# Involution: neighbourhoods laid out by the host and loaded raw, group norm applied behind the product

## The chip, the cores and the metric

The kernel runs on one core of a Trainium2 chip. The metric is the time on the device of one execution, in microseconds (us). The engines named below are PE (TensorE, matrix products), DVE (VectorE), ACT (ScalarE), POOL (GpSimd) and SP (SyncE, which here only issues DMAs). All data are 32-bit floats.

## The reference

Two layers on x of 8 images, 256 channels and 56 x 56 pixels. The first is an involution behind a group norm; the second is a block of two 3 x 3 convolutions with ternary weights and batch norms. The change lies in the first:

```python
ker = einsum('bchw,oc->bohw', gn(x), w_reduce) + b_reduce      # 256 -> 64
ker = einsum('bchw,oc->bohw', ker, w_span) + b_span            # 64 -> 16 * 49
xp = pad(gn(x), 3)
patches = stack([xp[:, :, i:i+H, j:j+W] for i in range(7) for j in range(7)])
x = x + (ker.reshape(B, 16, 1, 49, H, W)
         * patches.reshape(B, 16, 16, 49, H, W)).sum(axis=3)   # 16 groups of 16 channels
x = x + block(gn(x))                                           # the convolutions
```

Here `gn(v) = (v - m) / sqrt(s + 1e-5)`, with mean m and variance s of each image and each group of 8 channels. Every pixel has its own 7 x 7 kernel for each of 16 groups.

## The kernel before

The first stage works through 32 quarters (`quarters`, L984): an image b and 64 of its channels, c. The 128 partitions of a quarter are these 64 channels of the upper and of the lower half of the image, in the tile `xs[b, c]`. A quarter has ten rows of tiles (`ty`), each row seven tiles (`TX`) of 3 x 8 pixels (`PY`, `PX`) in both halves. A tile with its border is 9 x 14 = 126 pixels (`NQ`).

The product is done on PE with the pixels of the neighbourhood as the rows that are summed over. `q` is a tile of 126 neighbourhood pixels by 7 tiles by 128 channels. `a` (two buffers) holds for the same 126 pixels the kernels of each of the 24 output pixels, zero where the pixel lies outside its 7 x 7. `apply_row` (L861) makes one row with 28 products of `q` and `a`, and `pick_out` (L881) takes the channels of the right group out of its result (ACT L887, DVE L888, where `half_sb` is 1 or 0) and adds it to `xs` (POOL L891).

`generate` (L821) fills `a` for the next quarter, in 14 units: PE multiplies shifted windows of `wl` with `kr`, the reduced input (L842); `UNITS` says how many of a unit's positions ACT moves out of PSUM with the bias (L846), and DVE moves the rest (L851). `reduce` (L700) computes `kr` for the next image.

`q` needs the normalised pixels on partitions, while `xs` has the channels there. It comes in two ways. For four of the seven tiles (`NK`), `prep` (L755) writes the normalised input with its border to `xn` (POOL, `spread`, L734), transposes it on PE (L777), copies it to `stg` (ACT L780) and stores it in DRAM in `xtd` (SP L768); `load_q` (L797) loads 126 pixels by 512 values from there (SP L802). For the other three (`NX`), `surround` (L738) writes the bordered input to `xe` (POOL), with three rows of the other half from the host in `xa` (SP L743), and `transpose_q` (L805) transposes on PE (L809) and copies to `q` (ACT L812). The border must be zero after the norm; `xn`, `xe` and the ends of `xtd` are zeroed once.

The order on each engine is that of the text: `pin` (L924) ties every instruction to the one before it on its engine. In a row SP issues, in turn: stores of a finished quarter (`store_x1`, L903) or loads of the next image (L605), the stores that wait in `tasks`, then after `apply_row` the `load_q` that takes the buffer which this row frees (four buffers, `NQB`), and later the pieces of the convolutions' weights, which are quantised beside this stage (L294 loads, L323 stores to `wqd`). SP can't pass a DMA whose wait is not over.

After this stage come both convolutions (`conv_phase`, L355, with the products at L521) and an elementwise last stage (L1112).

## Time and profile before

| | |
|---|---|
| time before, median of 3 runs | 2253.05 us (2248.57 to 2256.51) |
| the profiled execution's own span | 2247.9 us |
| PE busy over the span | 1849.4 us (82%) |
| DVE busy | 1757.2 us (78%) |
| ACT busy | 1252.6 us (56%) |
| POOL busy | 580.1 us (26%) |
| moved by DMA | 411.28 MB |

The profile comes from one execution. A group of instructions is a line of the code with its engine, operation and tiles; beside it stand the number of instructions, the busy time, the mean time of one in ns, and the idle time of the engine just before them with what ended it. Busy times overlap between engines, so they don't add up to the span. In the waits, "SPq L802 <- PE pa L875" is time in which the DMA queue of SP stood at the DMA of L802 until an instruction of L875 on PE was done: total, times, longest. In a table of stretches each engine has its busy time and number of instructions in that stretch; then come the granted clock of PE (1.00 is full), the mean busy share of the 16 DMA engines, and GB/s.

### The profile page before, as it was taken

How to read it: one execution, taken by the hardware profiler on the slowest of the kernel's cores; microseconds unless marked ns; L12 is line 12 of the kernel's file. 1: busy time of each engine (PE TensorE's matmuls, PEld its weight loads, DVE VectorE, ACT ScalarE, POOL GpSimd, SP SyncE). 2: the span in 40 equal slices, each digit the busy share in tenths (PEclk: the TensorE clock that was granted, in tenths of full speed). 3: DMA queues.
4: the chain of work that ended last, by engine and by line, in shares of the span. 5: the costliest groups of instructions: out<-in, count | busy, mean ns of one | idle time of the engine just before them, and what ended most of it. 6: DMA issues, size and time to landing. Idle time of an engine off the chain costs nothing. (4 is left out here: it accounts for less than half of the span.)

```text
span 2247.9 us, 73156 instructions
## 1 busy us (share of the span) xinstructions
PE 1849.4 (82%) x31088; PEld 1701.1 (76%) x31088; DVE 1757.2 (78%) x3246; ACT 1252.6 (56%) x2417; POOL 580.1 (26%) x1320
## 2 busy tenths in 40 slices
PE   5989898898989889889889999999899999980000
PEld 4777777777877777778789999999899999980000
DVE  6767867678686776856589999998999999985444
ACT  3545555454554545556546766665576666663434
POOL 3536455464554645546400000000000000000000
PEclk9999999999999999999989999999899999995555
DMA  6647658475475755755453333334333333369999
GB/s 201 191 109 212 183 135 223 112 220 175 143 218 132 209 155 162 211 131 164 145 189 123 144 138 121 117 117 169 149 117 117 117 117 117 117 247 409 430 429 400
DMA packets 187588, 411.28 MB, mean 183 GB/s; under 512 B 77311, under 2 KB 93565, under 8 KB 179837
## 3 DMA queue, kind: packets, MB, share of 16 engines
q1 hardware_dynamic: 181664, 376.57, 51.3%
q10 hardware_dynamic: 5596, 30.03, 3.2%
q8 instruction: 245, 4.01, 0.8%
q14 instruction: 83, 0.67, 0.1%
HBM read 264.05 MB, written 142.48 MB: 181 GB/s over the span
## 5 line engine op out<-in xcount | busy, mean ns | idle before, releaser
L521 PE MATMUL c<-pl,wq 128*128 128x392 f32 x4608 | 858.1, 349 | 17.8 <-ACT pl L391 17.8
L521 PEld LDWEIGHTS c<-pl,wq 128*128 128x128 f32 x4608 | 856.1, 190 | 19.6 <-ACT pl L391 18.3
L851 DVE TENSOR_TENSOR a<-pg,bt 126x756 f32<-126x756 f32 (+3 forms) x640 | 392.2, 655 | 158.8 <-ACT a L846 122.4
L842 PE MATMUL pg<-kr,wl 64*126 64x140 f32 (+1 forms) x6144 | 447.6, 288 | 24.5 <-DVE a L851 14.2
L842 PEld LDWEIGHTS pg<-kr,wl 64*126 64x126 f32 x6144 | 385.2, 190 | 75.7 <-issue 42.8
L875 PE MATMUL pa<-a,q 126*32 126x48 f32 x17920 | 271.9, 207 | 61.9 <-issue 38.2
L875 PEld LDWEIGHTS pa<-a,q 126*32 126x32 f32 x17920 | 221.6, 111 | 115.2 <-issue 52.7
L846 ACT ACTIVATE a<-pg,bt 126x126 f32<-126x126 f32 x768 | 243.8, 476 | 98.4 <-PE pg L842 98.2
L891 POOL TENSOR_TENSOR x<-x,inv 128x168 f32<-128x168 f32 x320 | 165.8, 519 | 444.3 <-DVE inv L888 402.2
L391 ACT CAST pl<-r 128x812 fp32r<-128x812 f32 x192 | 162.5, 867 | 144.2 <-DVE r L386 125.9
L812 ACT COPY q<-ptq 126x384 f32<-126x384 f32 x320 | 138.3, 482 | 161.5 <-issue 91.7
L888 DVE SCALAR_TENSOR_TENSOR inv<-pa,half_sb,inv 128x168 f32<-128x168 f32 x320 | 116.6, 365 | 134.9 <-ACT inv L887 116.4
L371 POOL MEMSET xp<- 128x116 f32 x32 | 6.2, 195 | 828.0 <-DVE a L386 828.0
L392 DVE TENSOR_TENSOR pl<-r,pl 128x812 fp32r<-128x812 f32 x192 | 187.1, 1001 | 29.3 <-ACT pl L391 28.1
L734 POOL TENSOR_SCALAR xn<-x,gn 128x224 f32<-128x224 f32 (+2 forms) x384 | 175.5, 478 | 113.5 <-PE pt L777 62.2
L456 ACT ACTIVATE dummy<-y,nc 128x1568 f32<-128x1568 f32 (+1 forms) x128 | 200.1, 1563 | 4.8 <-DVE y L541 3.5
L734 POOL TENSOR_SCALAR xe<-x,gn 128x168 f32<-128x168 f32 (+2 forms) x384 | 161.5, 440 | 0.0
L780 ACT COPY stg<-pt 98x512 f32<-98x512 f32 x128 | 75.1, 587 | 131.5 <-issue 94.0
L150 DVE BATCH_NORM_STATS2 st<-x 128x6 f32<-128x392 f32 x256 | 138.3, 556 | 12.9 <-DMA x<-in_x 11.3
L809 PE MATMUL ptq<-ident_sb,xe 128*126 128x128 f32 x960 | 143.2, 284 | 6.0 <-DVE var_a L170 5.0
L887 ACT ACTIVATE inv<-pa,half_sb 128x168 f32<-128x168 f32 x320 | 128.5, 402 | 27.7 <-PE pa L875 24.9
L1071 ACT ACTIVATE xp<-raw,gn 128x392 f32<-128x392 f32 (+1 forms) x124 | 82.6, 721 | 62.6 <-DVE a L386 59.0
(153 smaller groups left out, 1896.6 us busy)
## 6 DMA issues: line engine op xcount, KB each, us to landing
q<-xtd SPq DMA_DIRECT2D x320, 252.0 KB
raw<-x1d SPq DMA_DIRECT2D x32, 812.0 KB
raw<-y1d SPq DMA_DIRECT2D x32, 812.0 KB
x<-in_x SPq DMA_DIRECT2D x64, 392.0 KB
xtd<-stg SPq DMA_DIRECT2D x128, 196.0 KB
x1d<-x SPq DMA_DIRECT2D x64, 392.0 KB
y1d<-y SPq DMA_DIRECT2D x30, 784.0 KB
y2d<-y SPq DMA_DIRECT2D x30, 784.0 KB
```

The costliest lines, as they stand in the source:

```text
L150: nc.vector.bn_stats(st[:, j, :], xt[:, j * NC:(j + 1) * NC])
L391: nc.scalar.copy(hi, r)
L392: nc.vector.tensor_tensor(lo, r, hi.bitcast(F32), ALU.subtract)
L456: nc.scalar.activation(dst, v, f, bias=shift[:, to:to + 1], accum_out=stats[:, to, j, n:n + 1])
L521: nc.tensor.matmul(ps[:, to, :NM], wq[k][:, t, dx, to * P:(to + 1) * P], part[:, t, :, dx:dx + W], start=(c == 0), stop=(c == last))
L734: nc.gpsimd.tensor_scalar(dst[:, i - d - k0:f - d - k0, :, x0:x0 + n], v[:, i:f, :, j0:j0 + n], scale, bias, ALU.mult, ALU.add)
L809: nc.tensor.transpose(pt[:NQ, k * P:(k + 1) * P], xe[c % 2][:, k, PY * ty:PY * ty + QY].rearrange("p r x -> p (r x)"), ident_sb)
L842: nc.tensor.matmul(dst, wl[rows, c, gp, o:o + NQ], kr[py][rows, px, :], start=True, stop=True)
L846: nc.scalar.activation(whole[:, g0 + i, p0 + j], ps[:NQ, i, j * nt:(j + 1) * nt], AF.Identity, bias=bt[:, c, g0 + i, p0 + j:p0 + j + 1])
L851: nc.vector.tensor_tensor(dst[:, g0:g0 + 2, p0:p0 + nv].rearrange("q g p t -> q g t p"), ps[:NQ, :, t0 * nv:t1 * nv].rearrange("q i (t p) ...
L875: nc.tensor.matmul(ps[o:o + 32, k * 2 * n:(k + 1) * 2 * n], q[:NQ, k, o:o + 32], av[:, t + k, g * 2 * n:(g + 1) * 2 * n], start=True, stop ...
L891: nc.gpsimd.tensor_tensor(xv, xv, iv.rearrange("p t (y x) -> p y t x", x=PX), ALU.add)
```

## The change

The host now lays out the neighbourhoods themselves: `x_nb` holds, for each quarter, raw input with a zero border, by column and row of the neighbourhood and then seven tiles by 128 channels. `load_q` loads all seven tiles of a row in one DMA (3584 B for each of 126 pixels). `prep`, `spread`, the old `surround`, `transpose_q`, `xtd`, `xn`, `xe` and `xa` are gone. The pixels of a neighbourhood are now counted by column first.

As `q` is raw, the norm is put behind the product. The scale is a factor in `pick_out` (`scale2` in place of `half_sb`). The mean gives a term for each pixel: minus mean times scale, times the sum of the pixel's 49 weights. `constant` makes it once for each quarter, as the first two steps of `generate`: the weights summed over 49 (`wsx`, and `bsum` for the bias; summed once at the start from `w_all` and `b_all`) times `kr` on PE, scale and shift on ACT, and an add to `xs` on POOL. A border pixel must then hold the channel's group mean: `params` makes a tile `rim` of means, and `load_rim` copies it with DMAs from SBUF to the border of each `q` after its load. There are two for the left and right columns of every row, and one more for each image row that lies outside, at `ty` = 0, 8 and 9. The new `surround` issues them when more than two loads (`PLEAD`) are without their border. `NQB` is 5 instead of 4, `ps_p` has three buffers instead of two, with `ps_one` in the buffers of `pa`, and in `UNITS` ACT takes ten positions of 24 instead of six.

```diff
@@ -40,27 +40,22 @@
 NE = 2 * TX
 QY, QX = PY + K - 1, PX + K - 1
 NQ = QY * QX
-LEAD = (PY - 1) * QX + PX - 1
+LEAD = (PX - 1) * QY + PY - 1
 WL = LEAD + NQ
-NK = 4
-NX = TX - NK
 HQ = TY * PY + K - 1
-RP = NK * P
-SR = HH // 4
-NSP = SR * QX
-UNITS = ((0, 3, 0), (3, 3, 0), (6, 2, 0), (8, 4, 2), (12, 4, 1), (16, 4, 2), (20, 4, 1))
+UNITS = ((0, 3, 0), (3, 3, 0), (6, 2, 0), (8, 4, 3), (12, 4, 2), (16, 4, 3), (20, 4, 2))
 NU = GP * len(UNITS)
 A_COLS = (NT * NP + NE * PX) * GQ
-PER_ROW = (2, 1, 2, 1, 2, 1, 2, 1, 2, 0)
-NQB = 4
-QLEAD = 2
+PER_ROW = (2, 2, 2, 1, 2, 2, 1, 2, 2, 0)
+NQB = 5
+PLEAD = 2
 NCB = 4
...
@@ -576,14 +571,14 @@
     with ExitStack() as ph1:
-        ps_p = ph1.enter_context(tc.tile_pool(name="ps_p", bufs=2, space=PSUM))
+        ps_p = ph1.enter_context(tc.tile_pool(name="ps_p", bufs=3, space=PSUM))
         ps_a = ph1.enter_context(tc.tile_pool(name="ps_a", bufs=2, space=PSUM))
...
         def ps_one(name):
-            return ps_a.tile([P, 512], F32, tag="pt", name=name)
+            return ps_a.tile([P, 512], F32, tag="pa", name=name)
...
@@ -618,17 +613,23 @@
             dst = small.tile([P, NCQ, 2], F32, tag="gn1", name=f"gn1_{b}")
-            yield from group_norm_params(mvs.pop(b), dst, ps_one, f"a{b}")
+            means = []
+            yield from group_norm_params(mvs.pop(b), dst, ps_one, f"a{b}", means)
...
-            edge = small.tile([P, 2, NCQ], F32, tag="gn1e", name=f"gn1e_{b}")
+            scale2 = small.tile([P, NCQ, 2], F32, tag="gn1s", name=f"gn1s_{b}")
             for j in range(2):
-                nc.vector.tensor_scalar(edge[:, j], dst[:, :, 1], side_sb[:, j:j + 1], None, ALU.mult)
-            prm[b], prm_edge[b] = dst, edge
+                nc.vector.tensor_scalar(scale2[:, :, j], dst[:, :, 0], half_sb[:, j:j + 1], None,
+                                        ALU.mult)
+            shift = small.tile([P, NCQ], F32, tag="gn1b", name=f"gn1b_{b}")
+            nc.vector.tensor_tensor(shift, dst[:, :, 1], bsum, ALU.mult)
+            dg = work.tile([P, NCQ, P], F32, tag="dg", bufs=1, name=f"dg_{b}")
+            for c in range(NCQ):
+                nc.gpsimd.tensor_scalar(dg[:, c], ident_sb, means[0][:, c, 0:1], None, ALU.mult)
             yield
             yield
             ps = ps_one(f"br_{b}")
@@ -638,6 +639,12 @@
                                      start=(c == 0), stop=(c == NCQ - 1))
             yield
             nc.vector.tensor_tensor(brn, br, ps[:, :1], ALU.add)
+            ps = ps_one(f"rim_{b}")
+            nc.tensor.matmul(ps[:NQ, :NCQ * P], ones[:, :NQ], dg.rearrange("p c f -> p (c f)"),
+                             start=True, stop=True)
+            rim = small.tile([P, NCQ, P], F32, tag="rim", name=f"rim_{b}")
+            nc.scalar.copy(rim[:NQ].rearrange("p c f -> p (c f)"), ps[:NQ, :NCQ * P])
+            prm[b] = dst, scale2, shift, rim
         def gn2_params(b0, b1):
...
@@ -666,7 +673,8 @@
-        xn = fixed([P, NK, SR, QX], "xn")
+        wsum, wsx = fixed([P, G], "wsum"), fixed([P, NCQ, CH], "wsx")
+        bsum, ones = fixed([P, NCQ], "bsum"), fixed([P, P], "ones")
@@ -677,19 +685,7 @@
-        side_sb = fixed([P, 2], "side_sb", side)
-        nc.gpsimd.memset(xn, 0.0)
-        xe = [fixed([P, NX, HQ, QX], f"xe{i}") for i in range(2)]
-        for v in xe:
-            nc.gpsimd.memset(v, 0.0)
-        zero = xn.rearrange("p k r x -> p (k r x)")
-        for d in (d for ds in xt_d for d in ds):
-            for r0, n in ((0, PAD), (PAD + HH, HQ - PAD - HH)):
-                e = n * QX * RP // P
-                nc.sync.dma_start(
-                    bass.AP(d[:].tensor, d[:].offset + r0 * QX * RP, [[e, P], [1, e]]), zero[:, :e])
+        nc.gpsimd.memset(ones, 1.0)
         nf = CT * 9 * C
...
-        def spread(dst, src, k0, nk, scale, bias):
...
-        def surround(b, c):
-            dst, p = xe[c % 2], prm[b]
-            around = work.tile([P, 2, PAD * W], F32, tag="xa", bufs=1, name=f"xa_{b}_{c}")
...
-        def prep(b):
...
-                for s in range(HH // SR):
-                    spread(xn, xs[b, c][:, s * SR * W:(s + 1) * SR * W], 0, NK,
-                           prm[b][:, c, 0:1], prm[b][:, c, 1:2])
-                    yield
-                    pt = ps_one(f"pt_{b}_{c}_{s}")
-                    for k in range(NK):
-                        nc.tensor.transpose(pt[:NSP, k * P:(k + 1) * P],
-                                            xn[:, k].rearrange("p r x -> p (r x)"), ident_sb)
-                    stg = work.tile([P, NK, P], F32, tag="stg", name=f"stg_{b}_{c}_{s}")
-                    nc.scalar.copy(stg[:NSP].rearrange("p k c -> p (k c)"), pt[:NSP, :RP])
-                    tasks.append(lambda stg=stg, s=s, store=store: store(stg[:NSP], PAD + s * SR))
...
         def load_q(b, c, ty):
             q = qpool.tile([P, TX, P], F32, tag="q", name=f"q_{b}_{c}_{ty}")
-            d = xt_d[b % 2][c][:]
-            src = bass.AP(d.tensor, d.offset + PY * ty * QX * RP, [[RP, NQ], [1, RP]])
-            nc.sync.dma_start(q[:NQ, :NK].rearrange("p k c -> p (k c)"), src)
+            nc.sync.dma_start(q[:NQ].rearrange("p k c -> p (k c)"),
+                              x_nb[b, c, :, PY * ty:PY * ty + QY, :])
             return q
-        def transpose_q(b, c, ty):
-            pt = ps_one(f"ptq_{b}_{c}_{ty}")
-            for k in range(NX):
-                nc.tensor.transpose(
-                    pt[:NQ, k * P:(k + 1) * P],
-                    xe[c % 2][:, k, PY * ty:PY * ty + QY].rearrange("p r x -> p (r x)"), ident_sb)
-            nc.scalar.copy(loads[b, c, ty][:NQ, NK:].rearrange("p k c -> p (k c)"),
-                           pt[:NQ, :NX * P])
+        def load_rim(b, c, ty):
+            q, rim = loads[b, c, ty], prm[b][3][:, c]
+            e = PAD * QY
+            for k, r0 in ((0, 0), (TX - 1, NQ - e)):
+                nc.sync.dma_start(q[r0:r0 + e, k], rim[r0:r0 + e])
+            for h in range(2):
+                for r in range(QY):
+                    y = h * HH + PY * ty + r - PAD
+                    if 0 <= y < H or r >= K - 1 + min(PY, HH - PY * ty):
+                        continue
+                    cols = slice(h * CH, (h + 1) * CH)
+                    nc.sync.dma_start(q[r:NQ:QY, :, cols],
+                                      rim[:QX, cols].unsqueeze(1).to_broadcast([QX, TX, CH]))
...
                     a[:NQ, n:].rearrange("q (t f) -> q t f", t=NE))
+        def constant(b, c):
+            n = (TY - 1) * TX
+            add = work.tile([P, NHW], F32, tag="add", bufs=1, name=f"add_{b}_{c}")
+            rows_of = [v[:, :(TY - 1) * PY * W].rearrange("p (t y w) -> p y t w", y=PY, w=W)
+                       for v in (add, xs[b, c])]
+            last = [v[:, (TY - 1) * PY * W:] for v in (add, xs[b, c])]
+            scale, bias = prm[b][0][:, c, 1:2], prm[b][2][:, c:c + 1]
+            for i0 in (0, 2):
+                ps = ps_tile(f"ks_{b}_{c}_{i0}")
+                for i in range(2):
+                    py = (i0 + i) % PY
+                    k0, m = (0, n) if i0 + i < PY else (NT, TX)
+                    rows = slice(i * CR, (i + 1) * CR)
+                    for h in range(2):
+                        nc.tensor.matmul(ps[h * CH:(h + 1) * CH, i, :PX * m], wsx[rows, c, :],
+                                         kr[py][rows, :, k0 + h * m:k0 + (h + 1) * m],
+                                         start=True, stop=True)
+                for i in range(2):
+                    py = i0 + i
+                    m = n if py < PY else TX
+                    src = ps[:, i, :PX * m]
+                    if py < PY:
+                        dst = rows_of[0][:, py].rearrange("p t (k x) -> p t k x", x=PX)
+                        src = src.rearrange("p (x t k) -> p t k x", x=PX, k=TX)
+                    else:
+                        dst = last[0].rearrange("p (k x) -> p k x", x=PX)
+                        src = src.rearrange("p (x k) -> p k x", x=PX)
+                    nc.scalar.activation(dst, src, AF.Identity, bias=bias, scale=scale)
+                for i in range(2):
+                    py = i0 + i
+                    v, x_ = (r[:, py] for r in rows_of[:2]) if py < PY else last
+                    nc.gpsimd.tensor_tensor(x_, x_, v, ALU.add)
+                yield
         def generate(b, c, a):
+            yield from constant(b, c)
             whole, rest = (v.rearrange("q t (g p) -> q g p t", g=GQ) for v in views(a))
             for u in range(NU):
                 gp, (p0, n, na) = u // len(UNITS), UNITS[u % len(UNITS)]
...
@@ -884,20 +850,26 @@
                          [:, :, h] for h in range(2))
             inv = work.tile([P, TX, NP], F32, tag="inv", bufs=3, name=f"inv_{b}_{c}_{ty}")
             iv = inv[:, :, :n]
-            nc.scalar.activation(iv, even, AF.Copy, scale=half_sb[:, 0:1])
-            nc.vector.scalar_tensor_tensor(iv, odd, half_sb[:, 1:2], iv, ALU.mult, ALU.add)
+            scale = prm[b][1][:, c]
+            nc.scalar.activation(iv, even, AF.Copy, scale=scale[:, 0:1])
+            nc.vector.scalar_tensor_tensor(iv, odd, scale[:, 1:2], iv, ALU.mult, ALU.add)
             y, m = ty * PY, n // PX
             xv = xs[b, c][:, y * W:(y + m) * W].rearrange("p (y t x) -> p y t x", t=TX, x=PX)
             nc.gpsimd.tensor_tensor(
                 xv, xv, iv.rearrange("p t (y x) -> p y t x", x=PX), ALU.add)
         queue = [(b, c, ty) for b in range(B) for c in range(NCQ) for ty in range(TY)]
-        loads = {}
+        loads, bare = {}, []
         def prefetch():
             if queue:
                 k = queue.pop(0)
                 loads[k] = load_q(*k)
+                bare.append(k)
+        def surround(keep=PLEAD):
+            while len(bare) > keep or bare and not queue:
+                load_rim(*bare.pop(0))
...
+        held = []
         qpool = ph1.enter_context(tc.tile_pool(name="qpool", bufs=NQB))
         pieces = ph1.enter_context(tc.tile_pool(name="pieces", bufs=1))
+        for _ in range(2):
+            held.append(qpool.tile([P, TX, P], F32, tag="q", name=f"sums{len(held)}"))
+        wv, bv = (t_.rearrange("p k c -> p (k c)")[:, :n_ * KK]
+                  for t_, n_ in zip(held, (G, NCQ)))
+        nc.sync.dma_start(wv, w_all)
+        nc.sync.dma_start(bv, b_all)
+        for dst, v in ((wsum, wv), (bsum, bv)):
+            nc.vector.tensor_reduce(dst, v.rearrange("p (g k) -> p g k", k=KK), AX.X, ALU.add)
+        nc.vector.tensor_copy(wsx.rearrange("p c (g i) -> p (c g) i", g=GQ),
+                              wsum.unsqueeze(2).to_broadcast([P, G, CH // GQ]))
         pin(start=True)
         for _ in params(0):
             pass
-        strips, around = prep(0), surround(0, 0)
...
         for py in range(PY):
-            next(strips)
-            transfer(len(tasks))
             reduce(0, py)
             for _ in range(2):
                 next(found)
+        for _ in range(NQB):
+            prefetch()
+        surround(0)
         for u, _ in enumerate(generate(0, 0, a_next)):
-            if u < 4 or u % 3 == 0 and u < 12:
-                next(strips)
-                transfer(len(tasks))
-            elif u < 9:
-                next(around)
             next(found, None)
             pin()
-            if u == 5:
-                for _ in range(NQB):
-                    prefetch()
-        for _ in around:
-            pass
         for _ in found:
             pass
...
@@ -1012,20 +982,12 @@
...
-                transfer(2)
                 row = apply_row(b, c, a, ty)
+                surround()
                 prefetch()
                 if r == PARAMS_AT:
                     norm = params(b + 1) if more else gn2_params(0, b)
-                if more and r == STRIPS_AT:
-                    strips = prep(b + 1)
-                if ty % 2:
-                    next(strips, None)
-                if ty % 2 == 0:
-                    for k in rows[m * TY + ty + QLEAD:m * TY + ty + QLEAD + 2]:
-                        transpose_q(*k)
                 next(norm, None)
                 if ty == 1 and last is not None:
...
@@ -1145,30 +1104,38 @@
                                     .reshape(B, NCQ, P, -1))
     xh = np.asarray(x)
-    around = np.zeros((B, C, 2, 2, PAD, W), np.float32)
-    around[:, :, 0, 1], around[:, :, 1, 0] = xh[:, :, HH:HH + PAD], xh[:, :, HH - PAD:HH]
+    xp = np.zeros((B, C, HQ + HH, TX * PX + K - 1), np.float32)
+    xp[:, :, PAD:PAD + H, PAD:PAD + W] = xh
+    s = xp.strides
+    near = np.lib.stride_tricks.as_strided(
+        xp, (B, NCQ, QX, HQ, TX, 2, CH),
+        (s[0], CH * s[1], s[3], s[2], PX * s[3], HH * s[2], s[1]))
...
-        "x_around": by_quarter(around),
+        "x_nb": np.ascontiguousarray(near).reshape(B, NCQ, QX, HQ, TX * P),
```

## The prediction

> **What bounds the kernel now.** I read the page first, then the busy time by stretches, the groups of instructions, and last the waits of the DMA queue (SP). The page's chain of waits has L521 of the convolutions and the DMAs of the last stage on it; the change touches neither. What changes is the involution stage, from the first L875 matmul at 61.5 us to the last at 1131.8: 32 quarters of ten rows, 1070.3 / 32 = 33.45 us a quarter.
>
> ```profile
> core 0: us, PE busy (x) PEld busy (x) DVE busy (x) ACT busy (x) POOL busy (x), PEclk, DMA share, GB/s
> 61.50:1131.80 1070.30, 955.65 (x26128) 816.04 (x26126) 768.73 (x2039) 572.40 (x1565) 550.91 (x1235) 0.98 0.61 171
> ```
>
> Per quarter, each divided by 32: PE 29.9, DVE 24.0, ACT 17.9, POOL 17.2 us. PE is busy 89% of the stage and is the bound; the DMA engines are 61% busy. The groups that the change touches:
>
> ```profile
> L842 PE MATMUL pg<-kr,wl 64*126 64x140 f32 (+1 forms) x6144 | 447.6, 288 | 24.5 <-DVE a L851 14.2
> L846 ACT ACTIVATE a<-pg,bt 126x126 f32<-126x126 f32 x768 | 243.8, 476 | 98.4 <-PE pg L842 98.2
> L891 POOL TENSOR_TENSOR x<-x,inv 128x168 f32<-128x168 f32 x320 | 165.8, 519 | 444.3 <-DVE inv L888 402.2
> L812 ACT COPY q<-ptq 126x384 f32<-126x384 f32 x320 | 138.3, 482 | 161.5 <-issue 91.7
> L780 ACT COPY stg<-pt 98x512 f32<-98x512 f32 x128 | 75.1, 587 | 131.5 <-issue 94.0
> L809 PE MATMUL ptq<-ident_sb,xe 128*126 128x128 f32 x960 | 143.2, 284 | 6.0 <-DVE var_a L170 5.0
> ...
> L777 PE MATMUL pt<-ident_sb,xn 128*98 128x128 f32 x480 | 77.3, 284 | 0.0
> ```
>
> (The last line is from the groups of PE in that stretch.) The reader is to see that transposes cost PE 143.2 + 77.3 us, and ACT copies 213 us behind them. SP issues every DMA of this stage in order, and its own waits are these:
>
> ```profile
> SPq L802 <- PE pa L875: 413.4, 185, 8.2
> SPq L294 <- DMA wqd<-piece_w: 103.9, 50, 4.5
> SPq L768 <- ACT inv L887: 50.0, 64, 1.2
> SPq L802 <- PE ptq L809: 23.3, 37, 1.9
> ```
>
> SP is early: at L802 it waits for PE to give a q buffer back, 413.4 + 23.3 us here and 21.3 more in two smaller rows (PE pg 15.6, PE pt 5.7), 458 in all, or 14.3 us a quarter. That is SP's reserve. A DMA costs SP:
>
> ```profile
> L802 SPq DMA_DIRECT2D q<-xtd x320: 307/323/2186, 49.0 to 1127.5; - x160
> ...
> L768 SPq DMA_DIRECT2D xtd<-stg x192: 307/521/2118, 34.3 to 1072.0; - x192
> ...
> L743 SPq DMA_DIRECT2D xa<-in_x_around x32: 356/368/1706, 48.5 to 1084.9; - x32
> ```
>
> (min/median/max ns.) What the DMA engines give, in three short stretches (columns as in the first fence): x loads of 3136 B rows; q loads alone, 2048 B rows; the start of a wqd store of 192 B pieces.
>
> ```profile
> 4.00:5.00 1.00, 0.00 (x0) 0.00 (x0) 0.21 (x1) 0.00 (x0) 0.00 (x0) 1.00 1.08 387
> 394.00:394.40 0.40, 0.40 (x53) 0.40 (x47) 0.40 (x3) 0.40 (x2) 0.00 (x0) 1.00 0.82 312
> 398.00:398.40 0.40, 0.40 (x9) 0.40 (x10) 0.40 (x2) 0.40 (x2) 0.00 (x0) 1.00 0.63 61
> ```
>
> And how long after the issue data can be used: wf is issued in two halves, and DVE gets the first at 29.35. The stretches of 1 us from 25 on moved 157, 369, 396 and 433 GB/s, so a half's 1.18 MB were there near 28.6, and about 0.75 us went on completion.
>
> ```profile
> 24.01 0.93 SPq L698 DMA_DIRECT2D wf<-in_w  x2
> ...
> 29.35 0.95 DVE L223 TENSOR_REDUCE cols<-wf 128x1 f32<-128x768 f32 x1 [3.93 <-DMA wf<-in_w]
> ```
>
> [...] The wf loads agree in kind (0.75 us after the last byte, and a q load issued at 408.58 moves its first bytes in the stretch 409.2 to 409.6, 0.6 to 1.0 us later).
>
> **The change, part by part,** per quarter, against the profiled run's 33.45 us.
>
> PE, removed: 30 ptq transposes at 143.2 / 960 = 0.149 us (4.5 us) and 16 pt at 77.3 / 480 = 0.161 (2.6), in all 7.1. Added: the term `constant`, six matmuls of 504 columns and two of 56, f32, 64 rows deep. L842 takes 447.6 / 6144 x 2 = 0.146 us for 140 columns (two instructions each, two row halves side by side), so 504 columns take 0.53 and the sum is 3.3 us; if four run side by side (row halves and column halves), half of it. I take 2.5, range 1.6 to 3.3. PE goes from 29.9 to 25.3.
>
> DVE: ACT takes ten of 24 positions instead of six. The 756-element form has a mean of 958 ns and the 504 form 679, 1.06 to 1.1 ns an element; four 756 pieces become 504 and four 504 become 252, so 8 x 0.27 = 2.2 us less. ACT: 16 more evacuations at 243.8 / 768 = 0.32 (5.1) and three activations of 504 elements near 0.7 (kr at L716 is 738 ns for 560) plus one small, 2.4; less 213.4 / 32 = 6.7 of copies. Together +0.8, 18.7. POOL loses 30 L734 operations (960 / 32) near 0.42 and gets three adds of 504 elements near 1.2 and a small one, about -8.6. None of the three becomes the bound, and all of them lie beside PE.
>
> So the engines alone would allow 25.3 / 0.89 = 28.4, or 25.3 plus today's 3.55 of PE idle time = 28.9. I take 28.9: 4.55 less. The third pair of PSUM banks helps PE by at most the 36 us in which L842, L875 and L711 wait for DVE a.
>
> SP, removed: six xtd stores at 0.52 to 0.7 (the tail up to 2.1 lifts the mean), their 1.8 us of waits on ACT (50.0 and 6.3, over 32), one xa at 0.37: 5.3 to 6.5, I take 5.9. Added: 20 rims of 27 partitions near 0.33 (6.6) and eight row rims of 14x7 pieces near 0.52 as xtd's edge stores (4.2): 10.8. And a wait that is not there today: at ty = 8, 9 and 0 the row rims overlap the two side rims, so L742 waits until both have landed; so 3 times a quarter SP stands still. Queued behind it are the next q load, x loads, x1d stores and piece fetches. Not seen in the trace, so from both sides: [...] 0.8 + 0.2 + 0.75 = 1.8 us (first byte, transfer, completion); with a q load and another transfer still ahead, 3.5. The q load is issued right before, so I take 2.6: 7.8. Net 10.8 + 7.8 - 5.9 = 12.7 more. SP's work without its reserve is 33.45 - 14.3 = 19.15 today and then 31.85 us a quarter, more than the 28.9 of PE. So where PE's stall goes, SP is late next.
>
> DMA engines: a q load grows from 252 to 441 KB[...]. x loads give 387 / 16 / 1.0 = 24.2 GB/s an engine[...]. Per row also x 0.21, x1d 0.25 (319 GB/s in the stretch 410.4 to 410.8), wqd 0.3, pieces 0.1. [...] I keep 31.85.
>
> Start: the 16 zero fills (11.18 us of SP) and the strips go, the loads of five rows and w_all come; the opening waits for the statistics and `kr` in both. I take 3 us less (0 to 8). Convolutions and last stage: nothing.
>
> Sum: 32 x 1.6 = 51, and 3: 2247.9 - 54 = 2194. The median of the runs, 2253.05, stands 5.15 above the profiled span: 2199.
>
> **The rivals.** (A) as above, 2199; its own range is 2140 to 2240 (a wait of 2.0 to 3.0). (B) SP hides it all: each wait is 1.6 or less, or the lead of two rows (5.8 us) absorbs the late rows; PE decides: 32 x 4.55 + 3 = 149, 2104. For it: SP waits 43% of the time today. Against: 28 DMAs more. (C) No change to be told from noise, a wait near 3.1. (D) Slower: the wait for side rims is 3.5, since the q load of 441 KB and often an x1d or wqd transfer lie ahead[...]. At 3.1 SP's reserve is used up; at 3.5 the quarter takes 33.45 - 14.3 + 10.8 + 10.5 - 5.9 = 34.55, 32 x 1.1 - 3 = +32, 2285. For it: [...] SP's issues already reach 2.1 us[...]; also PE's clock was 0.50 in the stretch 406.0 to 407.6 of today's trace, so gaps could cost twice. That the change doesn't do what it says is out: neither L777 nor L809 is left in its order of instructions.
>
> **Numbers.** Chances: A 0.40, B 0.17, C 0.06, D 0.37. The range of 2095 to 2300 takes in B and most of D; about 0.2 lies outside. A alone: 2140 to 2240. A difference under 0.3% (7 us) can't be told from none. Faster 0.57, same 0.06, slower 0.37.
>
> **What would show it.** Right: no L809/L777; PE busy falls by about 4.6 us a quarter; SP's wait for PE falls from 14.3 us a quarter to near nothing, with waits of L742 for DMA q of 2 to 3 us, 96 times; PE waits for DMA q at rows 8, 9 and 0. B: SP still waits for PE several us a quarter. D: a DMA share over 0.8 and PE idle over 8 us a quarter. Wrong altogether: if PE waits for ACT a or DVE a, or if the convolutions' time differs.

## The result, and the profile after

| | before | after |
|---|---|---|
| time, median of 4 runs each, taken together | 2250.81 us (2243.54 to 2256.51) | 2739.47 us (2736.0 to 2742.39) |
| ratio after to before | | 1.2173 (95% interval 1.2129 to 1.2217) |
| span of the profiled execution | 2247.9 us | 2734.2 us |
| involution stage, first to last product (L875, now L841) | 61.5 to 1131.8 us | 66.8 to 1620.6 us |
| one quarter (stage / 32) | 33.45 us | 48.56 us |

The kernel became 22% slower, and the forecast was 2199 us, 2.3% faster. "Side rims" are the two transfers a row that fill the left and right columns of the border; "row rims" are the eight a quarter that fill the lines outside the image, at `ty` = 8, 9 and 0. Of the 486 us that the span grew, 483.5 lie in the involution stage (1553.8 instead of 1070.3 us), so everything below is told per quarter. First the stretch of that stage in the kernel after (columns as in the prediction's first fence: length, busy time of each engine, granted clock of PE, DMA share, GB/s):

```profile
66.80:1620.60 1553.80, 973.54 (x25203) 796.41 (x25202) 741.24 (x2051) 583.36 (x1759) 306.25 (x473) 0.79 0.54 146
```

No engine is full: PE is busy 63% of the stage, DVE 48%, the DMA engines 54%. The clock fell from 0.98 to 0.79. So the stage waits for something that is not compute. The groups of instructions say for what (busy us, mean ns; then idle time ahead of the group and what ended it):

```profile
L841 PE MATMUL pa<-a,q 126*32 126x48 f32 x17920 | 329.1, 228 | 540.3 <-DMA q<-rim 479.6
...
L808 PE MATMUL pg<-kr,wl 64*126 64x140 f32 (+1 forms) x6144 | 489.6, 312 | 17.3 <-DVE a L817 10.5
...
L812 ACT ACTIVATE a<-pg,bt 126x126 f32<-126x126 f32 x1280 | 365.1, 483 | 172.1 <-PE pg L808 172.1
...
L783 POOL TENSOR_TENSOR x<-x,add 128x504 f32<-128x504 f32 (+1 forms) x128 | 126.3, 1018 | 61.9 <-ACT add L779 56.1
...
L766 PE MATMUL ks<-kr,wsx 64*64 64x504 f32 (+1 forms) x512 | 104.2, 812 | 0.0
```

The products wait 479.6 us, 15 us a quarter, for the border transfers (`rim`) to land in `q`. In the kernel before, their largest idle time was 38.2 us, for nothing that the profile shows ("issue"):

```profile
L875 PE MATMUL pa<-a,q 126*32 126x48 f32 x17920 | 271.9, 207 | 61.9 <-issue 38.2
```

The 30 + 16 transposes are gone as meant, and `constant` (L766) costs 104.2 / 32 = 3.26 us. Next the waits of SP's queue in that stage (total, times, longest):

```profile
SPq L742 <- DMA q<-rim: 236.8, 104, 4.6
SPq L726 <- PE pa L841: 62.0, 47, 23.5
SPq L726 <- PE pg L808: 58.2, 87, 3.4
SPq L289 <- DMA wqd<-piece_w: 36.7, 29, 2.5
```

SP's wait for PE to free a buffer, 14.3 us a quarter before, is down to 120.2 / 32 = 3.8 in this view, and to less in fact: 23.5 us are one wait that began before the stage, and in the 87 waits for L808 PE was done only after the issue of the q load had begun. Summed over SP's timeline in the stage, SP stands 62 us ahead of its q loads, at most 1.9 a quarter. The new wait of a row rim (L742) for the side rims takes 7.4. And what a DMA costs SP to issue (min/median/max ns), with who waited for what these lines brought:

```profile
L726 SPq DMA_DIRECT2D q<-in_x_nb x320: 807/858/1477, 17.2 to 1605.6; - x160
...
L735 SPq DMA_DIRECT2D q<-rim x640: 697/737/2116, 34.6 to 1613.9; - x160
...
  PE pa L841: 128.3, 90
...
L742 SPq DMA_DIRECT2D q<-rim x256: 802/832/1423, 37.4 to 1617.6; - x128
...
  PE pa L841: 351.3, 77
```

A side rim takes 0.74 us and a row rim 0.83, where the prediction had put 0.33 and 0.52. Even the shortest ones (0.70 and 0.80) are far above, so the price belongs to all of them and not to a few that were held up. The q load has become dearer too, from 0.32 us (L802) to 0.86; the prediction had no term for that. And of the 479.6 us that PE waits, 351.3 are waits for a row rim, which only rows `ty` = 8, 9 and 0 have: three rows in ten cost nearly three quarters of it. One such row in the chain of waits, in order of time (start, length, what; "DMA" is the time from issue to landing):

```profile
701.62 0.85 SPq L726
702.47 0.04 issue
702.52 0.54 SPq L600
703.06 0.05 issue
703.11 0.79 SPq L735
703.90 0.04 issue
703.95 4.18 DMA q<-rim
708.12 0.02 issue
708.14 0.02 SPq L742
708.15 0.03 issue
708.19 0.86 SPq L742
709.05 0.04 issue
709.09 0.83 SPq L742
709.93 0.04 issue
709.97 2.17 DMA q<-rim
712.14 0.14 issue
712.27 0.74 PE pa L841 x25
```

From the q load's issue at 701.62 to the product at 712.27 every microsecond hangs on the one before: the load and an x load, the side rims, 4.18 us until a side rim issued behind the 441 KB q load and the 392 KB x load has landed, then row rims (the last, of 24.5 KB, at 709.97), then 2.17 us until that has landed. SP itself issues nothing between the end of the second side rim's issue at 704.66 and the first row rim at 708.19; the next q load, behind the row rims in its order, comes at 710.88. The product before the one at 712.27 began at 702.98: 9.3 us for a row, where the mean row of the kernel before took 3.35.

### The profile page after: what moved, and what is told of

Its sections match the earlier page's. It is cut to its first block, busy times and chain, and to the rows that moved or that the text cites. A ratio compares the mean times of both kernels' runs of the same rounds, so it can differ in the third digit from the quotient of the medians.

```text
span 2734.2 us, 70931 instructions
## 1 busy us (share of the span) xinstructions
PE 1865.4 (68%) x30144; PEld 1679.0 (61%) x30144; DVE 1728.1 (63%) x3257; ACT 1263.8 (46%) x2617; POOL 319.3 (12%) x518
## 4 chain that ended last, share of the span: by engine, by line
PE 49%; DMA 25%; SPq 12%; DVE 6%; ACT 4%; issue 3%; POOL 1%; ACTq 0%; another core or an unknown queue 0%; DVEq 0%
PE c L516 31%; DMA q<-rim 16%; PE pg L808 7%; SPq L742 5%; PE pa L841 5%; DMA x1f<-x1d 4%; SPq L735 3%; ACT a L812 3%; PE ks L766 2%; SPq L726 2%; PE pk L707 2%; DVE a L817 1%; DMA wqd<-piece_w 1%; DMA y2f<-y2d 1%; DMA y1f<-y1d 1%
## 5 line engine op out<-in xcount | busy, mean ns | idle before, releaser
L841 PE MATMUL pa<-a,q 126*32 126x48 f32 x17920 | 329.1, 228 | 540.3 <-DMA q<-rim 479.6
L841 PEld LDWEIGHTS pa<-a,q 126*32 126x32 f32 x17920 | 276.1, 128 | 638.2 <-issue 367.6
L817 DVE TENSOR_TENSOR a<-pg,bt 126x504 f32<-126x504 f32 (+4 forms) x640 | 350.6, 583 | 297.8 <-ACT a L812 267.7
L808 PE MATMUL pg<-kr,wl 64*126 64x140 f32 (+1 forms) x6144 | 489.6, 312 | 17.3 <-DVE a L817 10.5
L808 PEld LDWEIGHTS pg<-kr,wl 64*126 64x126 f32 x6144 | 431.4, 214 | 47.4 <-issue 22.6
L812 ACT ACTIVATE a<-pg,bt 126x126 f32<-126x126 f32 x1280 | 365.1, 483 | 172.1 <-PE pg L808 172.1
L854 ACT ACTIVATE inv<-pa,gn1s 128x168 f32<-128x168 f32 x320 | 126.3, 395 | 677.0 <-PE pa L841 663.9
L855 DVE SCALAR_TENSOR_TENSOR inv<-pa,gn1s,inv 128x168 f32<-128x168 f32 x320 | 118.9, 371 | 490.6 <-ACT inv L854 489.5
L386 ACT CAST pl<-r 128x812 fp32r<-128x812 f32 x192 | 162.5, 868 | 138.8 <-DVE r L381 120.2
L783 POOL TENSOR_TENSOR x<-x,add 128x504 f32<-128x504 f32 (+1 forms) x128 | 126.3, 1018 | 61.9 <-ACT add L779 56.1
L1050 ACT ACTIVATE xp<-raw,bi_bn,sc_bn 128x392 f32<-128x392 f32 (+1 forms) x124 | 82.4, 721 | 58.7 <-DVE a L381 57.0
L766 PE MATMUL ks<-kr,wsx 64*64 64x504 f32 (+1 forms) x512 | 104.2, 812 | 0.0
L779 ACT ACTIVATE add<-ks,gn1b,gn 128x504 f32<-128x504 f32 (+1 forms) x128 | 78.3, 674 | 52.4 <-PE ks L766 49.2
L1081 DVE SCALAR_TENSOR_TENSOR y1f<-y2f,sc_bn,y1f 128x3136 f32<-128x3136 f32 (+2 forms) x20 | 56.6, 2830 | 63.9 <-DMA y2f<-y2d 53.5
```

The lines of the kernel that those rows point to most:

```text
L386: nc.scalar.copy(hi, r)
L766: nc.tensor.matmul(ps[h * CH:(h + 1) * CH, i, :PX * m], wsx[rows, c, :], kr[py][rows, :, k0 + h * m:k0 + (h + 1) * m], start=True, stop=True)
L808: nc.tensor.matmul(dst, wl[rows, c, gp, o:o + NQ], kr[py][rows, px, :], start=True, stop=True)
L812: nc.scalar.activation(whole[:, g0 + i, p0 + j], ps[:NQ, i, j * nt:(j + 1) * nt], AF.Identity, bias=bt[:, c, g0 + i, p0 + j:p0 + j + 1])
L817: nc.vector.tensor_tensor(dst[:, g0:g0 + 2, p0:p0 + nv].rearrange("q g p t -> q g t p"), ps[:NQ, :, t0 * nv:t1 * nv].rearrange("q i (t p) ...
L841: nc.tensor.matmul(ps[o:o + 32, k * 2 * n:(k + 1) * 2 * n], q[:NQ, k, o:o + 32], av[:, t + k, g * 2 * n:(g + 1) * 2 * n], start=True, stop ...
```

## The experiments

All times are of one run each unless an interval stands beside them; the kernel before, run beside them on the same chip, took 2243 to 2253 us. The changes are against the kernel after.

| run | us | us per quarter | PE clock | DMA share |
|---|---|---|---|---|
| before | 2250.8 | 33.45 | 0.98 | 0.61 |
| after | 2739.5 | 48.6 | 0.79 | 0.54 |
| e1, no border | 2297.4 | 34.7 | 0.89 | 0.67 |
| e2, side rims only | 2381.0 | 37.2 | | |
| e3, row rims only | 2356.1 | 36.7 | | |
| e8, nothing waits for side rims | 2528.6 | 41.8 | 0.82 | 0.61 |
| e9, side rims from HBM | 2685.6 | 46.9 | 0.79 | 0.55 |
| e12, q load in one piece | 2648.4 | 45.8 | 0.80 | 0.55 |
| e13, e8 + e9 + e12 | 2396.9 | 37.7 | 0.86 | 0.66 |
| e6, no border, 4 of 7 tiles loaded | 2208.2 | 32.0 | 0.93 | 0.53 |
| e11, no border, 1 of 7 tiles loaded | 2166.5 | 30.8 | 0.94 | 0.37 |

(Clock and share are of the involution stage of each run.)

**e1: no borders.**

```diff
-                load_rim(*bare.pop(0))
+                bare.pop(0)
```

> The changed kernel without load_rim: no DMA writes the borders, which stay zero instead of the group mean. Theory (SP is the bound: per quarter some 30 us to issue 10 loads at 0.86 and 28 border DMAs at 0.83, 7.4 us of standing wait before the row rims, 5 us of other issues): SP needs only 15 us a quarter, PE decides at 29 us a quarter instead of 48.6, about 2110 us in all. Rival 1 (the transfers themselves, 441 KB a row[...], are the bound): the loads stay, so over 2500. Rival 2 (the new work on PE, ACT and POOL is the bound): over 2500 as well, with PE waiting for ACT a or DVE a.

The borders account for 442 of the 489 us, or 13.9 us a quarter: most of the loss is theirs. But what is left is 34.7 and not the expected 29, so without any border the change would still have lost (2297 us beside 2249). That second miss is taken up at the end (e5, e6, e10, e11).

**e2 and e3: one kind of border alone.**

```diff
-            for k, r0 in ((0, 0), (TX - 1, NQ - e)):
-                nc.sync.dma_start(q[r0:r0 + e, k], rim[r0:r0 + e])
```

(e3; e2 leaves out the `dma_start` of L742 instead.)

> The changed kernel with the two side rims of each row, without the row rims at ty 0, 8 and 9 (those border pixels stay zero), so without the wait of one border DMA for another. Theory (issue time and wait together): 8 issues at 0.86 and 7.4 us of wait go, 48.6 - 14.3 = 34.3 us a quarter, 2280 us. Rival (the standing wait, and what it delays, is the whole loss; issue time is hidden): all comes back, 29 us a quarter, 2110.

> The changed kernel with the row rims alone, without the side rims (left and right border pixels stay zero); no border DMA waits for another. Theory: 20 issues at 0.82 and the wait go, SP has 25 us a quarter, PE decides, about 2110. Rival 1 (rims are late because the row rims land late behind the q load, whatever SP does): rows 0, 8 and 9 still stop PE, 2300 or more.

Side rims alone add 2.5 us a quarter to e1, row rims alone 2.0, both together 13.9. Issue prices did not change (0.73 and 0.81 us). e2 came out 2.9 us above its theory's 34.3. In e3 the rival's number held: PE still waits 94 us, 2.9 a quarter, for row rims, though no border waits for another. Each kind alone still fits largely beside PE; only with both is SP's queue nearly full, and only with both is there the wait at L742.

**e4: side rims over 126 partitions instead of 27** (whole columns are overwritten, with wrong values).

```diff
-            for k, r0 in ((0, 0), (TX - 1, NQ - e)):
-                nc.sync.dma_start(q[r0:r0 + e, k], rim[r0:r0 + e])
+            for k in (0, TX - 1):
+                nc.sync.dma_start(q[:NQ, k], rim[:NQ])
```

> The changed kernel with each side rim as one transfer of 126 partitions instead of 27 (it overwrites all pixels of the first and last tile, so these two tiles of a row are wrong). Order and waits are unchanged. Theory (the issue cost goes with the form of the transfer: 126 whole rows cost 0.32 at the old q load, 27 cost 0.74): an issue falls to 0.35, 48.6 - 20 x 0.47 = 39 us a quarter, 2430 us, although it moves 4.7 times the bytes. Rival (a copy from SBUF to SBUF is dear to issue): 0.74 or more an issue, 2735 or more.

2841.7 us, as the rival said. The issue took 0.79 us instead of 0.74: the small number of partitions is not what makes it dear.

**e7: POOL issues the borders.**

```diff
-                nc.sync.dma_start(q[r0:r0 + e, k], rim[r0:r0 + e])
+                nc.gpsimd.dma_start(q[r0:r0 + e, k], rim[r0:r0 + e])
```

(and the same at L742.)

> The changed kernel with all border DMAs issued by POOL instead of SP; the same transfers, the same waits, the result complete. Theory (the loss is SP's queue: issue time and standing waits): SP is as free as without borders, and the time comes to 2300 to 2360. Rival (a border lands late wherever it is issued): PE still waits hundreds of us for q, 2500 or more.

2696.7 us, within the rival's range. The waits moved with the work:

```profile
PE pa L841 <- DMA q<-rim: 339.3, 96, 10.5
...
POOL q L742 <- DMA q<-rim: 239.2, 74, 6.7
```

The wait for the side rims costs the new queue 239 us, as it cost SP 237, and there it also stands in front of POOL's own additions. Issue time can't be what holds this run: POOL issues a side rim in 0.51 us and a row rim in 0.61, and with these it is busy for 768 of the stage's 1513 us. From issue to landing a border takes 1.6 to 7.9 us there (median 3.6 and 3.5 us for the two kinds). So another queue alone doesn't cure it; the waits, the landings and the order of the queue are enough to hold PE.

**e8: row rims in tiles 1 to 5 only.** They no longer touch what the side rims write, so L742 has nothing to wait for.

```diff
-                    nc.sync.dma_start(q[r:NQ:QY, :, cols],
-                                      rim[:QX, cols].unsqueeze(1).to_broadcast([QX, TX, CH]))
+                    nc.sync.dma_start(q[r:NQ:QY, 1:TX - 1, cols],
+                                      rim[:QX, cols].unsqueeze(1).to_broadcast([QX, TX - 2, CH]))
```

> The row rims go into tiles 1 to 5 only, so that they no longer write where the side rims wrote, and nothing makes L742 wait for them: all 28 border transfers of a quarter are still issued, on the same queue (the border rows of the first and the last tile stay zero, which is left out of the result). Theory (the queue's issue time is the main loss, the standing wait a smaller one): only the 7.4 us per quarter of L742's wait go, 48.6 - 7.4 = 41.2 us per quarter, about 2490 to 2520 us, L735 and L742 still at 0.75 to 0.88 us each. Rival (the wait and what it holds up is the main loss; issuing would fit beside the products): 36 to 37 us per quarter as in the runs with one kind of border alone, about 2340 to 2380 us. If the wait is nothing: about 2735 us.

2528.6 us: 6.7 us a quarter less, of the 7.4 that the wait took. It is worth nearly its own length and no more, close to what the theory said; PE still waits 281.7 us for the landing of borders.

**e9: side rims read from HBM.**

```diff
-                nc.sync.dma_start(q[r0:r0 + e, k], rim[r0:r0 + e])
+                nc.sync.dma_start(q[r0:r0 + e, k], grp[r0:r0 + e])
```

> The side rims are read from a tensor in HBM of the same width (27 partitions of 512 bytes) instead of from the rim tile in SBUF; destinations, order and waits stay (the values in the border are then not the rims'). Theory A (an SBUF source is what makes these transfers dear to issue): L735 falls from 0.74 to about 0.32 us, 20 x 0.42 = 8.4 us per quarter less on SP's queue, about 40 us per quarter and 2440 to 2480 us. Theory B (27 partitions are the dear form, wherever they are read from): L735 stays at 0.7 to 0.8 us and the time at 2700 to 2760 us.

Here a theory on a price held and its consequence for the time did not. Of e9 first the issue prices of the side rims with PE's wait for them, and in the last line PE's wait for the row rims; then the waits of SP's queue:

```profile
L735 SPq DMA_DIRECT2D q<-in_grp x640: 273/337/2258, 29.5 to 1562.1; - x160
...
  PE pa L841: 105.3, 79
...
  PE pa L841: 337.7, 79
```

```profile
SPq L742 <- DMA q<-in_grp: 305.9, 102, 5.5
...
SPq L726 <- PE pa L841: 109.7, 82, 30.1
```

The median issue fell from 0.74 to 0.34 us (the mean, from SP's timeline, from 0.83 to 0.51: 6.4 us a quarter), so it is cheaper to issue from this source. Whether that is the memory or the layout was not separated: in HBM the 27 rows lie in one piece. An SBUF source alone isn't dear, as the `xtd` stores of the kernel before took 0.52 (the shortest 0.31). Yet the stage lost only 1.6. The wait at L742 grew by 69 us, or 2.2 a quarter, as it would if a side rim that is issued earlier lands no earlier behind the same q load. PE's wait for row rims hardly moved (351.3 before, 337.7 now). In the seven rows without row rims SP now waits longer for PE; the three dear rows gained little.

**e12: the q load in one piece.** The host lays out the 126 x 896 values of each row one behind the other.

```diff
-            nc.sync.dma_start(q[:NQ].rearrange("p k c -> p (k c)"),
-                              x_nb[b, c, :, PY * ty:PY * ty + QY, :])
+            nc.sync.dma_start(q[:NQ].rearrange("p k c -> p (k c)"), x_nb[b, c, ty])
```

> The changed kernel in every value; only the host lays each row's 126 x 896 neighbourhood out in one piece, so that the q load is a plain transfer, which took 0.32 us to issue in the run with row-first loads (0.86 in the changed kernel). If SP's sum of issue times sets the stage: 10 x 0.54 = 5.4 us per quarter less, 43.2 us per quarter, about 2565 us. If only the three rows with border rows set it: 1.6 to 2.5 us per quarter less, 2655 to 2690 us.

2648.4 us, 2.7 us a quarter less, a little more than the three rows alone were expected to give and half of what the sum would. The q load's mean issue time on SP's timeline fell from 0.86 to 0.47 us, 3.9 a quarter. PE's wait for row rims went from 351.3 to 306.2 us: this saving does lie ahead of the row rims in the dear rows, once a row.

**e13: e8, e9 and e12 together.**

> The plain q load, the side rims read from HBM, and the row rims in tiles 1 to 5 only, so that nothing waits for the side rims; all 28 border transfers of a quarter are issued (the values in the border are not the rims'). SP's sum: 49.5 - 5.4 - 6.5 - 7.4 = 30.2 us per quarter, below the 34.4 that the stage takes without borders: 34.5 to 36 us per quarter, 2280 to 2335 us. If the landing of the borders (3 to 4 us behind each q load) holds the products whatever SP does: above 38 us per quarter, 2400 us or more.

2396.9 us and 37.7 us a quarter, between the two and just short of the second. The gains of the parts, 6.7 + 1.6 + 2.7 = 11.0, add up to the 10.9 measured. PE's waits for borders (side rims, then row rims) are what remains:

```profile
  DMA q<-in_grp: 109.7, 70
...
  DMA q<-rim: 35.9, 38
```

SP waits for PE 179 us again, so its queue no longer binds throughout; waiting for borders still costs PE 4.6 us a quarter. Borders issued a row earlier (`PLEAD` 1) might hide that; it was not run with border DMAs.

**e5, e10, e6, e11: what is left without borders.** e5 counts the neighbourhood's pixels by row, which makes the q load one piece; e10 is e5 with `UNITS` as in the kernel before. e6 and e11 are e1 with only four tiles or one tile loaded and used for all seven (the line is that of e11; e6 has `k % 4`):

```diff
-                                         q[:NQ, k, o:o + 32],
+                                         q[:NQ, 0, o:o + 32],
```

> No border DMAs (border pixels stay zero), and the neighbourhood counted by row first as in the kernel before, so that a q load reads 126 whole rows that lie one after another instead of 14 columns of nine. Same bytes. Theory: the form sets the issue cost, 0.83 falls to about 0.33; SP is not the bound without borders (it waits 500 us for PE), so the time stays at that of the run without borders, 2297 (2275 to 2310). Rival (the dear form also slows the transfers and so PE): 2200 or less.

> The run with row-first loads and no borders (2284.5 us), with the units of the kernel before, in which ScalarE applies fewer of a tile's products and VectorE more (the border is left out). If the new split between ACT and DVE is part of why the stage takes 34.4 us per quarter without borders: 33 us or less, 2200 to 2250 us. If DVE is the tighter of the two: 2300 to 2340 us. If neither bounds the stage, but the instruction stream and the clock do: 2270 to 2295 us.

> No border DMAs, and each q load brings four of the seven tiles (252 KB, as before the change); PE multiplies the same four again for the other three, so all work on the engines stays and the result is wrong there. Theory (without borders the q traffic is what holds PE: its stream of instructions stops every 254 instructions, up to 4.0 us, as instructions come by the same DMA engines): PE's issue gaps in L841 and L808 fall from 114 us to about 45, the clock rises from 0.89 to 0.95 or more, 34.7 us a quarter become 29 to 30, 2140 us. Rival (the new order of work on PE, ACT and DVE is the limit): 2270 to 2300.

> No borders, and of the seven tiles of a q load only the first, which serves for all seven (products of the other tiles are then wrong): the same instructions on PE, ACT, DVE and POOL, a seventh of the q traffic. 7/7 took 34.4 to 34.7 us per quarter, 4/7 took 31.95. If the traffic is the cause of what stands above the predicted 28.9: about 29 to 30 us per quarter, 2110 to 2150 us, PE's gaps without a releaser near the 37 us of the kernel before, clock above 0.95. If the engines' chain is: 31.5 us per quarter or more, 2190 to 2210 us.

e5 (2284.5 us; its q load is issued in 0.32 us instead of 0.83) and e10 (2278.3) change almost nothing: neither SP's time nor the split between ACT and DVE holds the stage at 34.4. The traffic does for the most part: with all, four and one of seven tiles a quarter takes 34.7, 32.0 and 30.8 us, with the same instructions on PE. That is 3.9 of the 5.8 us by which e1 missed 28.9; both runs fell between what the theory and its rival expected. It shows on PE as stops without a releaser. In the timeline of e1 (start, length, group; in brackets the idle time before it):

```profile
508.69 0.99 PE L808 MATMUL pg<-kr,wl 64*126 64x140 f32 x13 [1.57 <-issue]
...
511.02 0.78 PE L841 MATMUL pa<-a,q 126*32 126x48 f32 x51
515.83 0.28 PE L841 MATMUL pa<-a,q 126*32 126x48 f32 x5 [4.03 <-issue]
```

PE stops for 4 us in the middle of a row's 56 products, with nothing to wait for. Where such stops follow each other (502.99, 508.69, 515.83 us), 127 and 128 products and as many weight loads lie between, some 256 instructions. The page of e1 has a DMA queue for instructions (packets, MB, share of the 16 engines):

```profile
q8 instruction: 238, 3.90, 0.7%
```

These are 238 packets of 16 KB; PE has 60,288 instructions, 253 for each packet. In the trace, all 68 stops of over 0.3 us without a releaser in e1's stage (112 us) end 1.2 to 1.7 us after such a packet has come in; by chance fewer than one in ten would. In the stage of the kernel before, all 42 (41 us) end 1.3 to 1.6 us after one, and in that of the kernel after 22 of 27 end 1.2 to 1.5 us after one. That PE stops because its instructions come late is the author's reading of this timing. What delays a packet no view shows, but the stops shrink with the q traffic. Over the run these stops before L841 and L808 take 114 us in e1, 55 in e6, 25 in e11 and 43 in the kernel before; of the 3.9 us a quarter between e1 and e11 they are 2.8. With e11, 1.9 us a quarter above the predicted 28.9 remain; `constant` explains 0.8 of them (3.26 for 2.5).

**Two versions without border transfers.** The rows are loaded by pixel row (e5) with a zero border, and POOL adds the rim to it through a mask, so that no border is a DMA any more:

```diff
+            v = q[:NQ, ::TX - 1]
+            nc.gpsimd.tensor_tensor(v, v, side[:NQ], ALU.add)
```

(and for the outer rows the same with a line of the rim.)

> Row-first loads as above, and the border is filled by an add on POOL (the host's border is zero, so the group mean is added there through a mask): no border DMA at all, four q buffers instead of five, the result complete. Theory: as the run without borders, 2280 to 2310, since POOL has room (14% busy without borders, 30 adds of 256 to 448 elements a quarter more). Rival (PE waits for POOL's adds): 2350 or more.

> The version whose border is added by POOL (2396.3 us), with the border added one row earlier. If PE's 199 us of waits for POOL's additions come from their being queued late: 2250 to 2330 us. If POOL itself is late because it serves the products' sums first: 2370 to 2400 us.

v1 takes 2396.3 us (ratio 1.0657, 95% 1.0592 to 1.0722). PE waits 199 us for POOL's additions. v2 adds the border one row earlier: 2316.3 us, and those waits are down to 49 us, so in v1 the additions came late in POOL's queue. For v1 the rival held, for v2 the first case. It is the fastest complete version with raw neighbourhoods that was run, and still slower than the kernel before (2243.2 beside it). No version found beats that kernel: even without any border the raw loads leave 2278.

## Why the prediction was wrong

- **What binds: right.** "SP late next", with a standing wait at L742 where the row rims overlap the side rims. SP's reserve of 14.3 us fell to at most 1.9, and L742 waits 2.28 us each time (236.8 / 104; the prediction's 2.6 was an estimate).
- **The cost of SP's issues: the step that failed.** "20 rims of 27 partitions near 0.33" and "eight row rims near 0.52" were borrowed from transfers between SBUF and DRAM; a copy from SBUF to SBUF had no row in the profile before, and the step gave it no upper bound. Summed over SP's timeline from 80 to 1600 us, a side rim took 0.826 us and a row rim 0.874, which is 20 x 0.50 + 8 x 0.35 = 12.7 us a quarter more than in the sum. A third price was left out without a reason: the q load keeps its place, but reads 14 x 9 pieces where it read one, and its mean issue rose from 0.46 to 0.86 us, 4.0 a quarter (e12 and e5 show that the layout makes it).
- **The sum over a quarter: right in kind, with these terms.** 31.85 + 12.7 + 4.0 - 0.4 (the wait at L742, 7.4 for 7.8) - 2.1 (the wait for stores to `wqd` fell from 103.9 us, at L294, to 36.7, now at L289) = 46.1 us of work for SP. With at most 1.9 of waiting for PE that is 48.0 of the 48.56. But a term taken away doesn't come back whole. In e9 6.5 us of issue time went, and the queue waited longer instead: 2.2 at L742, 1.5 ahead of the q loads, 0.8 at L289. 1.6 reached the time.
- **"The engines alone would allow 28.9": wrong, and enough to turn the sign alone.** Without borders it is 34.7. e6 and e11 show the missing term: the q load's traffic, judged by the DMA engines' share alone, slows PE itself (34.7, 32.0 and 30.8 us a quarter), most of it, 2.8 of the 3.9 us, in stops that end behind a packet of instructions. `constant` at 3.26 us was at the upper end given, and the clock of 0.89 (0.94 in e11) adds to PE's times: in the kernel after, 56 products took 0.80 us where 1.00 was granted (from 415.98) and 1.35 where 0.50 was (from 411.83).
- **DMA engines: they did not bind, as forecast.** The mean of all 16 is 0.54 x 48.56 = 26.2 us a quarter, and in e1 they moved 191 GB/s over the stage where they moved 146 here. What the busiest of them had was not shown.
- **DVE, ACT and POOL: nearly right.** Per quarter 23.2, 18.2 and 9.6 us, where 21.8, 18.7 and 8.6 followed from the sums. None binds.
- **Start: missed.** The first product comes 5.3 us later, not 3 earlier. No run looked for the cause.
- **Rival D, "slower", had the direction but not the cause.** It asked for waits of 3.5 us and a DMA share over 0.8; they were 2.28 and 0.54. Its other sign came: PE is idle for 18.1 us a quarter, where it named 8. Its 2285 us was far too low, as it used the same prices. Its remark that gaps could cost twice through the clock held in kind: the mean of the products went from 207 to 228 ns and that of L808 from 288 to 312, at a clock of 0.79. How much of the loss is the clock's was not separated.

## What to carry to other kernels

Price a DMA on the queue that issues it by its own form, and price it anew when its layout changes. Where the profile has no row for a form, bound it from above by the dearest row there is: 28 small copies at 0.8 us took 22 of a quarter's 48.6 us on the queue, though they moved 466 KB beside the 4410 KB of the q loads. Cost a stage by the rows that have the longest chain, not by the mean over a quarter: a saving in rows that have slack is not a saving, as e9 showed. A wait for one transfer in front of another, on a queue that is nearly full, costs nearly its length (e8: 6.7 of 7.4 us). And traffic that fits the DMA engines by its share can still slow the engine that it feeds (e1: share 0.67, 34.7 us a quarter; e11: 0.37, 30.8).

## What the runs showed of the hardware that was not expected

- Issue time on SP went with source and layout, not with the bytes: 27 partitions of 512 B took 0.74 us from SBUF and 0.34 from HBM, where they lie in one piece (e9); 126 partitions from SBUF 0.79 (e4); a q load of the same 441 KB took 0.86 as 14 x 9 pieces and 0.32 in one (e5). POOL issued the same 27 partitions from SBUF in 0.51 (e7). How far this holds for other forms is open.
- PE stopped for up to 4 us at steps of about 256 instructions (e1), all 68 times over 0.3 us until 1.2 to 1.7 us after a 16 KB packet of instructions had come in, and longer in all where the q loads moved more: 114 us at 191 GB/s (e1), 25 at 92 GB/s (e11).
- The granted clock of PE over the stage fell with its busy share: 0.98 at 89% (before), 0.89 at 81% (e1), 0.79 at 63% (after).
